# First cross-attention of a two-layer decoder: VectorE's instructions in written order, statistics and normalizations as steps of their own

## The chip, the cores and the metric

The kernel runs on one core of a Trainium2 chip, as one launch. A core has five engines with an instruction queue each: TensorE (PE, matrix products and transpositions), VectorE (DVE), ScalarE (ACT), GpSimd (POOL) and SyncE (SP), which here only issues DMA transfers. An engine works through its queue in order and waits on semaphores that other engines and transfers count up. The metric is the device time of one execution in microseconds (us), as the median of several runs; less is better.

## The reference, cut to what matters

The reference is two decoder layers on x of 16 batches x 112 tokens x 256 features. Each layer is `x + attention(norm(x))`, `x + cross_attention(norm(x), ctx)`, `x + ffn(norm(x))`. The change lies in the cross-attention of the first layer:

```
Q = (norm(x) @ W_Q + b_Q), K = (ctx @ W_K + b_K), V = (ctx @ W_V + b_V)   # 16 heads of 16
attn = softmax(Q K^T / sqrt(16));  out = (attn V) @ W_O + b_O;  x = x + out
```

The context has 375 rows a batch and is taken as it is. After this comes the first mixture of experts, which needs norm(x) of the result, router logits of it, and a shared expert; its shared expert and logits are computed inside the same stage. The second layer's cross-attention normalizes the same context; the mean and variance of each context row are worked out here already, and kept.

## The kernel before, in words

One stage handles the first cross-attention, about 154 to 572 us of the span. It loops over 16 batches b, and in each over four quads g, a quad being four heads. For a quad (b, g):

- `scores(b, g)`: four products of queries and keys (L614), each into a PSUM bank of its own, and on VectorE a negated maximum of each row (L616, tile mx).
- `shifted(b, g)`: TensorE transposes the maxima (L622), VectorE adds them to the queries (L624, tile qm).
- `weights(b, g, qm)`: the scores again, transposed and with the maxima taken off (L632), and ScalarE's exponential (L641).
- `values(b, g, pr)`: the products with V (L650), one quad behind.

While batch b is attended, batch b+1 is prepared: `prep(b + 1, part)` in quad `part` transposes the context and projects the queries (part 0, tile qn), the keys (part 1, tile kn), and the values (part 2). Queries and keys are then spread to 32-row groups (tiles qz and kz, two of each) by 16 small transfers each (`spread`, L554), all issued by SyncE; so is the context load (L224), two batches ahead. A batch thus takes 33 issues on SyncE. The tile cx has two buffers: a load waits until the batch two before it no longer needs its buffer.

In part 2, `prep` also takes the statistics of the context (L232 and L233 on VectorE into cmv, then two GpSimd instructions into cr). Quad 1 sets up `norm_one(lp, b + 2)`: statistics of x (L232, L233), GpSimd's power (L240, L241), the normalization (L236); the function that it returns, called in quad 3, transposes the result (L265, copied by L267 into xnT). `divide`, `out_T` and `out_proj` of batch b-1 follow in quads 1 to 3. `out_proj` adds the output to x (L687), and calls `norm_one` once more for the mixture of experts, into xrow; its transposition is put on the list `late` and taken in quad 1. A GpSimd add (L689) puts the normalized rows on x.

What sets the order: TensorE's is the order in which the Python loop calls things (`manual_schedule` with PE alone). The other engines' instructions are placed by a scheduler, which sorts by its own estimate of when each could start; each engine then keeps that order at run time. The next but one stage's instructions can be placed inside this one by it: the second layer's cross-attention loads its first two contexts into the same two cx buffers, and its normalization of them (L236, cx<-cx,cmv,cr) stands among this stage's VectorE instructions. PSUM is a pool of eight banks, used in turn: a TensorE step may have to wait until VectorE or ScalarE has read the bank of eight allocations before.

Of the kernel before, what the change touches and what calls it, by code (L numbers as in the profile page):

```python
# [20 lines left out]
NKC = S // KC  # L21
# [72 lines left out]
def tile_decoder(ctx: ExitStack, tc: tile.TileContext, t: dict, out: bass.AP):  # L94
# [135 lines left out]
    def stats_of(mv, src):  # L230
        st = sm.tile([src.shape[0], 6], F32, tag=f"st{src.shape[0]}", name="st", bufs=4)
        nc.vector.bn_stats(st, src)  # L232
        nc.vector.bn_aggr(mv, st)  # L233
# [4 lines left out]
    def rstd_pow(r, var):  # L238

        nc.gpsimd.tensor_scalar(r, var, EPS_LN, None, ALU.add)  # L240
        nc.gpsimd.tensor_tensor(r, r, power[: r.shape[0], : r.shape[1]], ALU.pow)  # L241

    def norm_one(lp, b, keep=None, affine=None, dst=None):


        if keep is None:
            mv = sm.tile([L, 2], F32, tag="nmv", name="nmv", bufs=4)
            r = sm.tile([L, 1], F32, tag="nr", name="nr", bufs=4)
        else:
            mv, r = keep[0][:, b, :], keep[1][:, b : b + 1]  # L250
        xn = lp.tile([L, D], F32, tag="xn", name="xn", bufs=2) if dst is None else dst
        stats_of(mv, x[:, b, :])
        rstd_pow(r, mv[:, 1:2])
        normed(xn, x[:, b, :], mv[:, 0:1], r)
        if affine is not None:
            mv2 = sm.tile([L, 2], F32, tag="nmv", name="nmv", bufs=4)
            r2 = sm.tile([L, 1], F32, tag="nr", name="nr", bufs=4)
            stats_of(mv2, xn)
            rstd_pow(r2, mv2[:, 1:2])
            normed(xn, xn, mv2[:, 0:1], r2)  # L260

        def to_xnT():
            pt = bank()
            for c in range(2):
                nc.tensor.transpose(pt[:, c * L : (c + 1) * L], xn[:, c * 128 : (c + 1) * 128], ident[:L, :L])  # L265
            if affine is None:
                nc.vector.tensor_copy(  # L267
                    xnT[:, :, b * L : (b + 1) * L], pt[:, : 2 * L].rearrange("p (c l) -> p c l", l=L)
                )
            else:  # L270
                for c in range(2):
                    nc.scalar.activation(
                        xnT[:, c, b * L : (b + 1) * L],
                        pt[:, c * L : (c + 1) * L],
                        AF.Identity,
                        bias=vec(affine[1] + c),
                        scale=vec(affine[0] + c),
                    )

        return to_xnT  # L280
# [247 lines left out]
    with ExitStack() as ph:  # L528
# [29 lines left out]
        def prep(b, part):  # L558
            if part == 0:
                if b + 2 < B:  # L560
                    cxs[b + 2] = load_ctx(b + 2)
                cT = lp.tile([128, 2, S], F32, tag="cT", name="cT", bufs=1)
                for c in range(2):
                    pt = bank()
                    for j in range(NKC):
                        nc.tensor.transpose(
                            pt[:, j * KC : (j + 1) * KC],
                            cxs[b][:, j, c * 128 : (c + 1) * 128],
                            ident[:KC, :KC],
                        )  # L570
                    nc.scalar.copy(cT[:, c, :], pt[:, :S])
                cTs[b] = cT
                nc.gpsimd.tensor_add(x[:, b, :], x[:, b, :], bo2[:, 1, :])
                qn = lp.tile([128, 2, L], F32, tag="qn", name="qn", bufs=1)
                pq = bank()
                for hf in range(2):
                    mm_sum(
                        pq[:, hf * L : (hf + 1) * L],
                        [(wq[:, c, hf * 128 : (hf + 1) * 128], xT(c, b)) for c in range(2)],
                    )  # L580
                for hf in range(2):
                    nc.vector.tensor_scalar(
                        qn[:, hf, :], pq[:, hf * L : (hf + 1) * L], vec(hf), 0.25, ALU.add, ALU.mult
                    )
                spread(qz[b % 2], qn)
            if part == 1:
                cT = cTs[b]
                kn = lp.tile([128, 2, S], F32, tag="kn", name="kn", bufs=1)
                for hf in range(2):
                    pk = bank()  # L590
                    mm_sum(pk[:, :S], [(wk[:, c, hf * 128 : (hf + 1) * 128], cT[:, c, :]) for c in range(2)])
                    nc.scalar.activation(kn[:, hf, :], pk[:, :S], AF.Identity, bias=vec(2 + hf), scale=1.0)
                spread(kz[b % 2], kn)
            if part == 2:
                cT = cTs.pop(b)
                for j in range(NKC):
                    pv = bank()
                    mm_sum(pv[:KC, :D], [(cT[:, c, j * KC : (j + 1) * KC], wv[:, c, :]) for c in range(2)])
                    nc.vector.tensor_tensor(
                        va[b % 2][:, j, :, :16],  # L600
                        pv[:KC, :D].rearrange("p (h d) -> p h d", d=16),
                        bV.rearrange("p (h d) -> p h d", d=16),
                        ALU.add,
                    )
                cx = cxs.pop(b)
                for j in range(NKC):
                    stats_of(cmv[:, b * NKC + j, :], cx[:, j, :])
                rstd_pow(cr[:, b * NKC : (b + 1) * NKC], cmv[:, b * NKC : (b + 1) * NKC, 1])

        def scores(b, g):  # L610
            ps = [bank() for _ in range(4)]
            for i in range(4):
                r = slice(32 * i, 32 * i + 32)
                mm(ps[i][:L, :S], qz[b % 2][r, g, :], kz[b % 2][r, g, :], start=True, stop=True)  # L614
            for i in range(4):
                nc.vector.tensor_reduce(  # L616
                    mx[b % 2][:, g, i, 16:17], ps[i][:L, :S], AX.X, ALU.max, negate=True
                )
# [65 lines left out]
        def out_proj(b, oT):  # L684
            po = bank()
            mm_sum(po[:L, :D], [(oT[:, c, :], wo[:, c, :]) for c in range(2)])
            nc.vector.tensor_add(x[:, b, :], x[:, b, :], po[:L, :D])  # L687
            late.append(norm_one(None, b, dst=xrow[:, b, :D]))
            nc.gpsimd.tensor_add(x[:, b, :], x[:, b, :], xrow[:, b, :D])  # L689

        late = []

        def logits(b):
            pl = bank()
# [19 lines left out]
                xb = x[:, b : b + 2, :].rearrange("p b d -> p (b d)")  # L714
                nc.vector.tensor_add(xb, xb, po[:L, :])

        with tc.manual_schedule(engines={mybir.EngineType.PE}):
            normq = {b: norm_one(lp, b) for b in range(2)}
            normq.pop(0)()
            normq.pop(1)()  # L720
            for part in range(3):
                prep(0, part)
            scores(0, 0)
            quads = [(b, g) for b in range(B) for g in range(NQ)]
            behind, oT = None, {}
            for n, (b, g) in enumerate(quads):
                if b + 1 < B and g < 3:
                    prep(b + 1, g)
                if b + 2 < B and g == 1:
                    normq[b + 2] = norm_one(lp, b + 2)  # L730
                if b + 2 < B and g == 3:
                    normq.pop(b + 2)()
                if b:
                    if g == 1 and late:
                        late.pop(0)()
                    if g == 2 and b > 1:
                        logits(b - 2)
                    if g == 1:
                        divide(b - 1)
                    if g == 2:  # L740
                        oT[b - 1] = out_T(b - 1)
                    if g == 3:
                        out_proj(b - 1, oT.pop(b - 1))
                qm = shifted(b, g)
                if n + 1 < len(quads):
                    scores(*quads[n + 1])
                pr = weights(b, g, qm)
                if behind is not None:
                    values(*behind)
                behind = (b, g, pr)  # L750
            a0 = shared_up(0)
            values(*behind)
            late.pop(0)()
            a1 = shared_up(1)
            divide(B - 1)
            shared_down(0, a0)
            logits(B - 2)
            oT = out_T(B - 1)
            a2 = shared_up(2)
            out_proj(B - 1, oT)  # L760
            shared_down(1, a1)
            shared_down(2, a2)
            late.pop(0)()
            logits(B - 1)
            a3 = shared_up(3)
            shared_down(3, a3)
# [704 lines left out]
```

## Time and profile before

| what | value |
|---|---|
| median of 3 runs | 1873.21 us (1871.97 to 1875.34) |
| profiled execution, its own time | 1875.62 us |
| its span, first to last instruction | 1873.8 us |
| mean granted TensorE clock | 0.942 |
| busy over the span | PE 1631.8, DVE 969.3, ACT 603.9, POOL 520.5 us |
| busy from 200 to 530 us (330 us of this stage) | PE 291.76, DVE 207.39, ACT 125.41, POOL 50.99 us |
| granted clock in those 330 us | 0.97 |

A line of the timeline gives the start in us from the span's beginning, the busy time, the engine (PEld is TensorE's weight load, SPq SyncE's DMA issue), the line of the kernel, the operation, output and input tiles, shapes, and how many were merged; in brackets how long the engine was idle just before, and what released it. In the list of waits a line names who waited, for whom, the total, how often, and the longest. SyncE's time in the profile is the issuing of a transfer, not its movement. Busy TensorE is not TensorE at its peak: the clock granted may be half of full speed.

### The profile page before, as it was taken

The numbers are of one execution on the slowest core, as the hardware profiler recorded it, in microseconds if no ns is written. First come the engines' busy times: TensorE is split into PE (matmuls) and PEld (weight loads), VectorE is DVE, ScalarE is ACT, GpSimd is POOL, SyncE is SP. The second block draws the span as 40 slices with busy tenths as digits, with TensorE's granted clock in tenths as the row PEclk, the third lists the DMA queues.
The fourth block names the chain that finished last, engine by engine and source line by source line (L and its number), as shares of the span: only waits on it lengthen the run. The fifth ranks groups of instructions, "written<-read, shape, count | busy, mean of one in ns | idle before, by whom it ended". The sixth has DMA issues, their size and how long they took to land. (4 is left out here: it accounts for less than half of the span.)

```text
span 1873.8 us, 31175 instructions
## 1 busy us (share of the span) xinstructions
PE 1631.8 (87%) x11755; PEld 1226.3 (65%) x11755; DVE 969.3 (52%) x2637; ACT 603.9 (32%) x1440; POOL 520.5 (28%) x699
## 2 busy tenths in 40 slices
PE   5877888898892496899999899999997999979992
PEld 4765666666661374778787566666665888868882
DVE  6864566666653243877776555655455432222222
ACT  2330334333430252223322334334342333313330
POOL 5532111111103452333333343534443000030003
PEclk9987899999996698999999999999998999999996
DMA  9401111111102345100000100000001244453422
GB/s 266 137 1 44 46 36 42 38 42 40 40 20 81 108 143 194 50 1 1 1 1 1 40 17 11 24 9 20 15 9 45 74 147 147 157 186 134 161 85 65
DMA packets 93342, 125.60 MB, mean 67 GB/s; under 512 B 17761, under 2 KB 76298, under 8 KB 93194
## 3 DMA queue, kind: packets, MB, share of 16 engines
q1 hardware_dynamic: 85178, 107.88, 18.7%
q0 software_dynamic: 5184, 13.13, 2.3%
q10 hardware_dynamic: 2832, 2.60, 0.5%
q8 instruction: 95, 1.56, 0.4%
q14 instruction: 53, 0.43, 0.1%
HBM read 94.40 MB, written 21.18 MB: 62 GB/s over the span
## 5 line engine op out<-in xcount | busy, mean ns | idle before, releaser
L1193 POOL TENSOR_SCALAR pr<-pr,den 112x375 f32<-112x375 f32 x128 | 156.3, 1239 | 197.7 <-DVE den L1191 191.7
L1373 DVE SCALAR_TENSOR_TENSOR hT<-pT,vT,gt 128x264 f32<-128x264 f32 x128 | 62.9, 492 | 242.3 <-ACT gt L1372 242.2
L115 PE MATMUL pT<-xnT,w_all 128*128 128x224 f32 (+2 forms) x736 | 163.4, 374 | 6.2 <-DVE xnT L267 6.2
L115 PEld LDWEIGHTS pT<-xnT,w_all 128*128 128x128 f32 x736 | 132.9, 196 | 25.0 <-issue 13.9
L641 ACT ACTIVATE pr<-pT 125x336 f32<-125x336 f32 x256 | 94.6, 456 | 167.8 <-PE pT L632 167.8
L1410 POOL DMA_INDIRECT got<-eo,row x32 | 30.4, 949 | 393.1 <-PE pT L115 215.4
L616 DVE TENSOR_REDUCE mx<-pT 112x1 f32<-112x375 f32 x256 | 125.7, 539 | 21.7 <-PE pT L614 21.0
L115 PE MATMUL pT<-cT,w_all 128*128 128x375 f32 x384 | 136.4, 496 | 0.2 <-ACT cT L1142 0.2
L115 PE MATMUL pT<-w_all,cT 128*125 128x256 f32 (+1 forms) x384 | 135.0, 495 | 0.0
L115 PE MATMUL pT<-hT,w_all 128*128 128x264 f32 x512 | 119.5, 392 | 6.4 <-ACT hT L1378 6.4
L115 PE MATMUL pT<-w_all 128*128 128x264 f32 x512 | 120.5, 392 | 0.0
L115 PE MATMUL pT<-e1T,w_all 128*128 128x264 f32 x512 | 119.1, 392 | 0.0
L115 PEld LDWEIGHTS pT<-hT,w_all 128*128 128x128 f32 x512 | 99.0, 194 | 24.2 <-ACT hT L1378 6.8
L1090 POOL TENSOR_TENSOR pr<-pr,den 112x448 f32<-112x448 f32 x64 | 59.3, 948 | 197.6 <-DVE den L1088 140.6
L115 PEld LDWEIGHTS pT<-e1T,w_all 128*128 128x128 f32 x512 | 98.4, 193 | 16.9
L115 PEld LDWEIGHTS pT<-w_all 128*128 128x128 f32 x512 | 98.2, 193 | 16.7
L115 PEld LDWEIGHTS pT<-cT,w_all 128*128 128x128 f32 x384 | 72.6, 194 | 53.1 <-issue 13.7
L115 PE MATMUL pT<-w_all,oT 128*112 128x256 f32 x448 | 106.4, 383 | 0.0
L115 PE MATMUL pT<-w_all,xnT 128*112 128x256 f32 (+1 forms) x320 | 103.8, 472 | 0.9 <-ACT xnT L390 0.9
L115 PEld LDWEIGHTS pT<-w_all,cT 128*125 128x125 f32 x384 | 70.9, 191 | 45.0 <-issue 31.8
L1372 ACT ACTIVATE gt<-pT,vT 128x264 f32<-128x264 f32 x128 | 61.4, 481 | 115.2 <-PE pT L115 92.4
L1182 ACT ACTIVATE pr<-pT,top 112x375 f32<-112x375 f32 x128 | 72.4, 573 | 52.1 <-DVE top L1181 50.1
(247 smaller groups left out, 3020.4 us busy)
## 6 DMA issues: line engine op xcount, KB each, us to landing
w_all<-in_L_ffn_w_c_fc_dram SPq DMA_DIRECT2D x16, 1024.0 KB
w_all<-in_L_ffn_w_gate_dram SPq DMA_DIRECT2D x16, 1024.0 KB
w_all<-in_L_ffn_w_c_proj_dram SPq DMA_DIRECT2D x16, 1024.0 KB
cx<-in_ctx_dram SPq DMA_DIRECT2D x32, 375.0 KB
kz<-kn SPq DMA_DIRECT2D x256, 23.4 KB
xg<-fill SPq DMA_DIRECT2D x1, 5547.0 KB
xb<-xg SPq DMA_DIRECT2D x43, 129.0 KB
eo<-os SPq DMA_DIRECT2D x16, 264.0 KB
```

The costliest lines, as they stand in the source:

```text
L115: mm(o, l, r, start=(i == 0), stop=(i == len(terms) - 1))
L616: nc.vector.tensor_reduce(mx[b % 2][:, g, i, 16:17], ps[i][:L, :S], AX.X, ALU.max, negate=True)
L641: nc.scalar.activation(pr[:, i, :], pw[i][:KC, : NKC * L], AF.Exp)
L1090: nc.gpsimd.tensor_tensor(pr[:, k], pr[:, k], bcast(den[:, k, :], L), ALU.mult)
L1182: nc.scalar.activation(pr[:, i, :], ps[i][:L, :S], AF.Exp, bias=top[:, i : i + 1], scale=1.0, accum_out=den[:, i : i + 1],)
L1193: nc.gpsimd.tensor_scalar(pr[:, n, :], pr[:, n, :], den[:, n : n + 1], None, ALU.mult)
L1372: nc.scalar.activation(gt, ps[1][:, :HS], AF.Identity, bias=vec(n_v + e * NJ + j), scale=1.0)
L1373: nc.vector.scalar_tensor_tensor(hT[:, j, :], ps[0][:, :HS], vec(12 + e * NJ + j), gt, ALU.add, ALU.mult)
L1410: nc.gpsimd.indirect_dma_start(out=got[:, :], out_offset=None, in_=eo[b // HB][:, :], in_offset=bass.IndirectOffsetOnAxis(ap=row[k][:, b : ...
```

## The change

VectorE's order in this stage becomes the order of the calls too (`manual_schedule` gets DVE beside PE). For that `norm_one` is taken apart into steps, and each is called at a place of its own:

- `stats(b)`: L232, L233 and the two GpSimd instructions; `norm(b)`: the normalization; `norm_T(b)`: transposition and copy to xnT; `out_norm(b)`: the normalization into xrow and the GpSimd add.
- `ctx_stats(b)`: the context's statistics, taken out of `prep(b, 2)`. For batch 0 it stands after the first scores; for b+1 behind the maxima that quad 2 of b issues.
- Within a quad the steps are called behind `scores` of the next quad: statistics of b+2 and `out_norm(b - 2)` in quad 0, `norm(b + 2)` in quad 1, `ctx_stats(b + 1)` in quad 2, `stats(b - 1)` in quad 3.
- `norm_T(b - 2)` moves into quad 1 with one batch more of delay for the output's normalization: its statistics are taken in quad 3 of the batch after, its normalization in quad 0 of the next.
- At the start `norm_T(1)` moves behind `prep(0, 0)`; at the end `shared_down(2, a2)` moves behind `norm_T(B - 1)`.

The instructions are the same in number and kind. Instructions of other stages are still placed by the scheduler, on VectorE too.

```diff
-                cx = cxs.pop(b)
-                for j in range(NKC):
-                    stats_of(cmv[:, b * NKC + j, :], cx[:, j, :])
-                rstd_pow(cr[:, b * NKC : (b + 1) * NKC], cmv[:, b * NKC : (b + 1) * NKC, 1])
+        def ctx_stats(b):
+            cx = cxs.pop(b)
+            for j in range(NKC):
+                stats_of(cmv[:, b * NKC + j, :], cx[:, j, :])
+            rstd_pow(cr[:, b * NKC : (b + 1) * NKC], cmv[:, b * NKC : (b + 1) * NKC, 1])
+
+        mvs, xns = {}, {}
+        def stats(b):
+            mv = sm.tile([L, 2], F32, tag="nmv", name="nmv", bufs=4)
+            r = sm.tile([L, 1], F32, tag="nr", name="nr", bufs=4)
+            stats_of(mv, x[:, b, :])
+            rstd_pow(r, mv[:, 1:2])
+            mvs[b] = mv, r
+
+        def norm(b, dst=None):
+            mv, r = mvs.pop(b)
+            xn = lp.tile([L, D], F32, tag="xn", name="xn", bufs=2) if dst is None else dst
+            normed(xn, x[:, b, :], mv[:, 0:1], r)
+            xns[b] = xn
+
+        def norm_T(b):
+            xn = xns.pop(b)
+            pt = bank()
+            for c in range(2):
+                nc.tensor.transpose(pt[:, c * L : (c + 1) * L], xn[:, c * 128 : (c + 1) * 128], ident[:L, :L])
+            nc.vector.tensor_copy(xnT[:, :, b * L : (b + 1) * L], pt[:, : 2 * L].rearrange("p (c l) -> p c l", l=L))
+
+        def out_norm(b):
+            norm(b, dst=xrow[:, b, :D])
+            nc.gpsimd.tensor_add(x[:, b, :], x[:, b, :], xrow[:, b, :D])
...
-            late.append(norm_one(None, b, dst=xrow[:, b, :D]))
-            nc.gpsimd.tensor_add(x[:, b, :], x[:, b, :], xrow[:, b, :D])
-
-        late = []
...
-        with tc.manual_schedule(engines={mybir.EngineType.PE}):
-            normq = {b: norm_one(lp, b) for b in range(2)}
-            normq.pop(0)()
-            normq.pop(1)()
-            for part in range(3):
-                prep(0, part)
+        with tc.manual_schedule(engines={mybir.EngineType.PE, mybir.EngineType.DVE}):
+            stats(0)
+            stats(1)
+            norm(0)
+            norm_T(0)
+            norm(1)
+            prep(0, 0)
+            norm_T(1)
+            prep(0, 1)
+            prep(0, 2)
             scores(0, 0)
+            ctx_stats(0)
...
                 if b + 1 < B and g < 3:
                     prep(b + 1, g)
-                if b + 2 < B and g == 1:
-                    normq[b + 2] = norm_one(lp, b + 2)
-                if b + 2 < B and g == 3:
-                    normq.pop(b + 2)()
+                if g == 1 and b > 1:
+                    norm_T(b - 2)
+                if g == 3 and b + 2 < B:
+                    norm_T(b + 2)
                 if b:
-                    if g == 1 and late:
-                        late.pop(0)()
...
                 qm = shifted(b, g)
                 if n + 1 < len(quads):
                     scores(*quads[n + 1])
+                if g == 0:
+                    if b + 2 < B:
+                        stats(b + 2)
+                    if b > 1:
+                        out_norm(b - 2)
+                if g == 1 and b + 2 < B:
+                    norm(b + 2)
+                if g == 2 and b + 1 < B:
+                    ctx_stats(b + 1)
+                if g == 3 and b:
+                    stats(b - 1)
                 pr = weights(b, g, qm)
...
+            out_norm(B - 2)
             a0 = shared_up(0)
             values(*behind)
-            late.pop(0)()
+            norm_T(B - 2)
...
             out_proj(B - 1, oT)
+            stats(B - 1)
             shared_down(1, a1)
+            out_norm(B - 1)
+            norm_T(B - 1)
             shared_down(2, a2)
-            late.pop(0)()
```

## The prediction

> **What bounds the kernel now.** The page's slices and the chain that ended last speak for the whole span; the change lies in one stage, 154 to 572 us. So I read the stage's waits, then the timeline of one batch, then the timeline of SyncE alone. The list of waits (200 to 540 us; total us, times, longest) names what holds VectorE and TensorE:
>
> ```profile
> DVE st L232 <- DMA cx<-in_ctx_dram: 41.6, 12, 5.6
> PE pT L265 <- DVE mx L616: 19.7, 10, 3.5
> PE pT L566 <- DVE mx L616: 7.6, 13, 0.6
> PE pT L632 <- DVE qm L624: 8.8, 12, 0.7
> ```
>
> VectorE waits 12 times for a context load. The timeline of a batch (start, us, engine, line) shows what is queued behind that wait:
>
> ```profile
> 301.09 0.92 PE L632 MATMUL pT<-qm,kz 32*125 32x112 f32 x24 [0.74 <-DVE qm L624]
> ...
> 306.53 0.43 DVE L232 BATCH_NORM_STATS2 st<-cx 125x6 f32<-125x256 f32 x1 [4.22 <-DMA cx<-in_ctx_dram]
> 306.87 0.53 DVE L616 TENSOR_REDUCE mx<-pT 112x1 f32<-112x375 f32 x1
> ...
> 307.46 0.41 PE L265 MATMUL pT<-call,xrow 112*128 112x112 f32 x2 [2.02 <-DVE mx L616]
> ```
>
> The fourth maximum stands behind statistics of a context still in flight, and TensorE stands 2.02 us behind that maximum. With the 0.74 and the 0.6 of L566, TensorE loses about 3.4 us of a batch of 23.2. Removing these looks like 14 x 3.4 = 48 us. But SyncE decides what can be kept:
>
> ```profile
> 300.87 0.42 SPq L224 DMA_DIRECT2D cx<-in_ctx_dram  x1
> 301.39 11.09 SPq L554 DMA_DIRECT2D qz<-qn  x16
> 312.58 10.37 SPq L554 DMA_DIRECT2D kz<-kn  x16
> 323.06 0.42 SPq L224 DMA_DIRECT2D cx<-in_ctx_dram  x1
> 324.12 12.06 SPq L554 DMA_DIRECT2D qz<-qn  x16
> ```
>
> It issues 33 transfers a batch with no pause. Each needs 0.63 us (0.587 and a gap of 0.045), some 1 to 1.8. From 185.5 (first qz of batch 1) to 510.6 (batch 15) a period is 325.2/14 = 23.2 us. Idle gaps over 0.1 us in SyncE's timeline sum to 11.7. Of these 6.2 lie ahead of the first qz of a batch (1.19, 0.12, 1.75, 0.57, 0.90, 0.21, 0.16, 1.33), waiting for qn; 5.5 lie inside runs and come from transfers. A batch's first scores need the fourth kz, which lands 1.3 us after its issue; they follow that landing by -0.4 to 3.4 us. SyncE is a second bound right behind TensorE.
>
> The last lines concern the next stage's context, which the scheduler normalizes here (L236):
>
> ```profile
> 510.12 0.42 SPq L224 DMA_DIRECT2D cx<-in_ctx_dram  x1
> ...
> 516.28 0.41 DVE L236 TENSOR_SCALAR cx<-cx,cmv,cr 125x256 f32<-125x256 f32 x1 [5.45 <-DMA cx<-in_ctx_dram]
> ...
> 517.21 0.41 PE L265 MATMUL pT<-call,xrow 112*128 112x112 f32 x2 [3.48 <-DVE mx L616]
> ...
> 532.64 0.32 PE L622 MATMUL pT<-call,mx 112*128 112x112 f32 x1 [1.54 <-DVE mx L616]
> ```
>
> It is issued as soon as kz of batch 14 is done, VectorE waits 5.45 us, TensorE 3.48.
>
> **The Trainium skill.** "DVE: scalar operands, raw-bit mode, write accounting and state across instructions" (Flops that outlive an instruction) says the vector queue is one in-order queue; the trace agrees: maxima whose scores are ready stand 4.2 us behind a waiting instruction. "Perfetto Trace Analysis" (What "DMA-bound" means) names a sequencer full of DMA slices as a bound of its own; SyncE above agrees. "TensorE: Matmul & The Clock Gate" (What's actually happening) lets the clock fall to half after an idle window of some 3.4 us; the trace agrees: TensorE idles 3.3 us until 192.1, and the slice 192 to 196 has clock 0.50.
>
> **The change, part by part.** I use the order of instructions in the compiled changed program; its times are from the rows above.
>
> *Steady part.* Statistics of a context (three L232 of 0.4 us, three L233 of 0.17) now belong to the context one batch ahead, which landed long before. Statistics of x and the normalization are a quad apart, which covers the 1.0 us of GpSimd's power. Ahead of qn stand only four maxima and one L232/L233. All three waits go. What comes instead: context statistics (1.7 us) stand ahead of qm of the fourth quad, whose matmuls wait about 1.1 us for it. TensorE's own pace becomes 23.2 - 3.4 + 1.1 = 20.9 us; SyncE's floor is (325.2 - 6.2)/14 = 22.8. So SyncE bounds and only its qn waits go: -6.2. At the start qn(0) no longer stands behind context statistics: first matmuls end at 163.0, qn at 163.4 rather than 164.1: -0.7. kz of batch 14, finished at 510.0 before, is finished at 503.1.
>
> *The two hoisted loads.* A context buffer is free only after its statistics, so the scheduler sets every context load one place later in SyncE's order. The next stage's first load (batch 0) comes after kz(14), its second after kz(15). But VectorE has their L236 early:
>
> ```
> SyncE:   kz(14) x16 | cx' 0 | qz(15) x16 | kz(15) x16 | cx' 1
> VectorE: qm(13,3) | L236 cx' 0 | mx(14,0) x2 | L236 | mx x2 | L232 | L236 | L233 | qn(15) x2
> VectorE: qm(14,3) | mx(15,0) x1 | L236 cx' 1 | mx x2 | L236 | mx x1 | L232 | L236 | L233 | qm(15,0)
> ```
>
> mx(14,0) can start when the fourth kz(14) has landed, but stands behind a load that is issued after the sixteenth. No deadlock: kz needs nothing of VectorE. First stall: from the end of kz(14), issue 0.1, landing 5.6 (5.3 to 6.7 in this stage, one early load at 7.4), L236 and first maximum 1.0; then TensorE does values 0.78, six transposes 1.1, projection 1.15 for batch 15; qn and signals 0.55: 10.3 us until the first qz(15), against 0.6 before (510.02 to 510.64): +9.7. TensorE has then idled some 11 us, so its three steps run at half clock, as at 180 to 194 us (1.35, 1.5, 1.9): +1.7.
>
> Batch 15's 32 issues then run with no load just ahead: 32 x 0.63 and one long one, 21.3 against 22.65 before: -1.3.
>
> Second stall: from the end of kz(15), 0.1 + 5.6, then L236, two maxima, L236, one maximum: 2.3. The transposition of mx(15,0) starts 8.0 after that end; before, it started 0.65 ahead of it (532.64 against 533.29): +8.7. TensorE is idle about 10 us and restarts at half clock; after the idle time up to 192.1 this lasted to 197.8, so 5.7 us at half cost 2.9: +2.9. From here TensorE alone sets the end.
>
> *Tail.* In the last batch no projection covers out_norm(13), which now stands behind four maxima: xrow is 1.0 us late for L265 and delays the next qm: +1.2. At the end norm_T(15) waits behind one shared_down instead of two: +0.5. Later stages have the same order on every engine and shift as a whole; the xb fetches behind the second load wait for routing anyway.
>
> Sum: -6.2 - 0.7 + 9.7 + 1.7 - 1.3 + 8.7 + 2.9 + 1.7 = +16.5 us. The profiled execution took 1875.6 (span 1873.8), so it would take 1892.1; the median of the runs stands 2.4 below it: 1889.7.
>
> Unknown: GpSimd's and ScalarE's order hardly changes and is costed at nothing; both idle most of the stage (51 and 125 us busy of 330), and even 1 us late they stand behind SyncE's slack of 1.9 us a batch. Gaps inside SyncE's runs could shrink too, by 5.5 at most; or the qn waits stay: 6.2 back. Half clock: 0 to 7 for both stalls together, I take 4.6.
>
> **Rivals.**
> 1. *Stalls as worked out, SyncE's stream no faster.* The statistics ahead of qm and SyncE's uneven issues meet, and the period stays at 23.2. For it: TensorE's margin is only 1.9 us. Against: qn has nothing slow ahead of it. 16.5 + 6.2 = +22.7: 1895.9.
> 2. *Smaller stalls.* The clock stays full (4.6 less) and gaps inside the runs go too (5.5 less): +6.4: 1879.6. For it: 5.45 us of waiting at 516 cost only one half-clock window of 3.4 us. Against: the idle times are now twice as long.
> 3. *Faster.* The two loads do not stand in the way. Then SyncE gives 6.9, and the last batch, whose scores lagged the landing by 2.8 us, gives 1.5 more: about 1865. One mechanism decides: L236 must find its data. The load would have to be issued 12 us earlier (seven for the twelve kz behind the fourth, 5.6 for landing), before kz(14). The compiled order says otherwise.
> 4. *No difference:* stalls of about 4 us each, as before; needs the load six us ahead of kz's end.
>
> **How the numbers follow.** Forecast 0.62 (1884 to 1894), rival 1 0.12, rival 2 0.16, rival 3 0.07, rival 4 0.03. A measurement of this kernel tells 0.2%, 3.7 us. Rivals 1 and 2 are slower too: slower 0.90, same 0.03, faster 0.07. The range 1880 to 1896.5 runs from rival 2 to rival 1.
>
> **What would show it.** L232 of cx waits for no load; L265 and qm waits gone from the list; SyncE without gaps ahead of qz up to batch 14; kz(14) finished near 503. Then L236 idle before it about 10 us twice, followed by TensorE idle over 8 us and clock 0.5, qz(15) near 515 and the stage ending some 16 us later. Wrong if the L236 waits are under 6 us, if SyncE still pauses ahead of qz, or if kz(14) ends past 508.

## The result, and the profile after

The changed kernel takes 1883.85 us (median of 22 runs, 1879.10 to 1892.43), the kernel before beside it 1874.24 (22 runs, 1870.00 to 1884.66): a ratio of 1.0053, 95% interval 1.0040 to 1.0065, so about 10 us slower. The forecast was 1889.7 with a range of 1880 to 1896.5.

The profiled execution of the changed kernel took 1879.71 us (span 1877.9), which is below its median by 4.1, that of the kernel before 1875.62, which is above its own by 1.4. So the two profiles lie only 4.1 us apart. Part of what they lack against the 9.6 us between the medians is scatter outside the change: over all kernels of this study the first transposition of the self-attention (L491) comes at 37.4 to 41.0 us, and the program behind this stage takes 1300.3 to 1303.4 us; the changed kernel's profile has the lowest value of both, together 3.1 us less than the profile of before.

In the code of the changed kernel the maxima are L645, their transposition L651, qm L653, scores L643 and L661, values L679. Its list of waits, 200 to 545 us (who waited for whom: total us, times, longest), answers to the list of before:

```profile
DVE cx L236 <- DMA cx<-in_ctx_dram: 23.1, 2, 13.6
PE pT L679 <- DVE mx L645: 10.5, 1, 10.5
PE pT L651 <- DVE mx L645: 10.4, 1, 10.4
PE pT L643 <- DMA kz<-kn: 9.2, 9, 1.7
PE pT L661 <- DVE qm L653: 5.0, 18, 0.9
```

The 41.6 us that L232 waited for loads are gone, and so are the waits for a maximum at the transpositions. Two single waits stand in their place, and a new small one: TensorE now waits for the keys (kz), which are SyncE's transfers. The timeline shows the two large ones with what is behind them (start, us, engine, line; idle time and its releaser in brackets):

```profile
497.26 0.41 SPq L224 DMA_DIRECT2D cx<-in_ctx_dram  x1
502.81 0.41 DVE L236 TENSOR_SCALAR cx<-cx,cmv,cr 125x256 f32<-125x256 f32 x1 [13.56 <-DMA cx<-in_ctx_dram]
503.74 1.35 PE L679 MATMUL pT<-pr,va 125*32 125x112 f32 x24 [10.54 <-DVE mx L645]
...
508.46 10.28 SPq L554 DMA_DIRECT2D qz<-qn  x16
...
518.84 10.37 SPq L554 DMA_DIRECT2D kz<-kn  x16
...
529.31 0.42 SPq L224 DMA_DIRECT2D cx<-in_ctx_dram  x1
535.02 0.41 DVE L236 TENSOR_SCALAR cx<-cx,cmv,cr 125x256 f32<-125x256 f32 x1 [9.57 <-DMA cx<-in_ctx_dram]
...
537.18 0.45 PE L651 MATMUL pT<-call,mx 112*128 112x112 f32 x1 [10.41 <-DVE mx L645]
```

Each load is issued right behind the last kz, VectorE stands at L236 until it has landed (5.5 and 5.7 us), and TensorE idles over 10 us each time. The SyncE timeline of the changed kernel shows what bounds the batches ahead of it:

```profile
312.97 0.42 SPq L224 DMA_DIRECT2D cx<-in_ctx_dram  x1
314.03 11.34 SPq L554 DMA_DIRECT2D qz<-qn  x16
325.46 11.44 SPq L554 DMA_DIRECT2D kz<-kn  x16
337.01 0.40 SPq L224 DMA_DIRECT2D cx<-in_ctx_dram  x1
```

It issues almost without a pause, as before. The mean period over batches 1 to 13 is 22.85 us, against 23.21 before.

The steps of the prediction can be laid beside the two profiles (us from the span's start; the last column adds up the prediction's terms):

| moment | before | after | difference | predicted |
|---|---|---|---|---|
| last transposition of the self-attention (L491) | 136.0 | 130.7 | -5.3 | 0 |
| first qz | 164.19 | 156.73 | -7.5 | -0.7 |
| kz(14) finished | 510.02 | 497.16 | -12.9 | -6.9 |
| qz(15) starts | 510.64 | 508.46 | -2.2 | +4.5 |
| kz(15) finished | 533.29 | 529.21 | -4.1 | +3.2 |
| transposition of mx(15,0) | 532.64 | 537.18 | +4.5 | +11.9 |
| end of the stage (last addition of the shared expert) | 571.33 | 577.61 | +6.3 | +16.5 |

From row to row the predicted differences hold within 1 us, but for the first two rows and the last: the stage starts 7.5 us early where 0.7 was expected, and its end adds 1.7 where 4.6 were expected.

That gain lies ahead of the stage. In the kernel before, the scheduler had put the context statistics of batches 0 and 1 (six L232, L233, and GpSimd's L240 and L241) into the first self-attention. Its timeline there:

```profile
55.06 0.42 DVE L232 BATCH_NORM_STATS2 st<-cx 125x6 f32<-125x256 f32 x1
...
57.95 0.41 PE L491 MATMUL pT<-call,a 112*128 112x112 f32 x2 [1.10 <-POOL a L484]
...
63.65 0.89 POOL L241 TENSOR_TENSOR cr<-cr,power 125x3 f32<-125x3 f32 x1
...
64.50 0.72 POOL L484 TENSOR_TENSOR a<-a 112x256 f32<-112x256 f32 x1
65.28 0.41 PE L491 MATMUL pT<-call,a 112*128 112x112 f32 x2 [1.46 <-POOL a L484]
```

The same transposition in the changed kernel, whose written order holds these statistics in their own stage:

```profile
56.18 0.41 PE L491 MATMUL pT<-call,a 112*128 112x112 f32 x2 [0.29 <-POOL a L484]
...
62.35 0.41 PE L491 MATMUL pT<-call,a 112*128 112x112 f32 x2 [0.29 <-POOL a L484]
```

A batch of the self-attention takes 6.2 us there instead of 7.3, because VectorE and then GpSimd (L484) have nothing foreign ahead of what TensorE waits for.

### The profile page after: what moved, and what is told of

Same layout as the page of the kernel before. It is cut to its first block, busy times and chain, and to the rows that moved or that the text cites. A ratio compares the mean times of both kernels' runs of the same rounds, so it can differ in the third digit from the quotient of the medians.

```text
span 1877.9 us, 31401 instructions
## 1 busy us (share of the span) xinstructions
PE 1648.7 (88%) x11755; PEld 1241.6 (66%) x11755; DVE 975.0 (52%) x2637; ACT 603.7 (32%) x1440; POOL 520.8 (28%) x699
## 5 line engine op out<-in xcount | busy, mean ns | idle before, releaser
L115 PEld LDWEIGHTS pT<-xnT,w_all 128*128 128x128 f32 x736 | 137.6, 205 | 24.1 <-issue 14.6
L645 DVE TENSOR_REDUCE mx<-pT 112x1 f32<-112x375 f32 x256 | 124.3, 541 | 26.1 <-PE pT L643 23.2
L115 PEld LDWEIGHTS pT<-e1T,w_all 128*128 128x128 f32 x512 | 97.5, 192 | 16.5
L115 PEld LDWEIGHTS pT<-cT,w_all 128*128 128x128 f32 x384 | 72.7, 195 | 53.1 <-issue 11.6
L643 PE MATMUL pT<-kz,qz 32*112 32x375 f32 x512 | 80.8, 541 | 14.8 <-DMA kz<-kn 14.8
## 6 DMA issues: line engine op xcount, KB each, us to landing
kz<-kn SPq DMA_DIRECT2D x256, 23.4 KB
```

The source lines that it names most:

```text
L115: mm(o, l, r, start=(i == 0), stop=(i == len(terms) - 1))
L645: nc.vector.tensor_reduce(mx[b % 2][:, g, i, 16:17], ps[i][:L, :S], AX.X, ALU.max, negate=True)
```

## The experiments

The theory: (1) two stalls of L236 behind late context loads cost about 21 us; (2) SyncE's issuing bounds the batches in both kernels, so little of VectorE's gain is kept; (3) the start gains some 7 us because no context statistics stand in the self-attention. The rival to each stands in the expectations. Times are medians. Each group of runs had runs of the kernel before beside it (1874.88 for the first four, 1873.58 for the next four, 1875.05 for the last two); at the ratio 1.0053 the changed kernel is at 1884.8 and 1883.5 beside the first two groups.

### The two stalls, both and one

```diff
-                for j in range(NKC):
-                    n = b * NKC + j
-                    normed(cxs[b][:, j, :], cxs[b][:, j, :], cmv[:, n, 0:1], cr[:, n : n + 1])
+                with tc.issue_after(last[0]) if b in (0, 1) else ExitStack():
+                    for j in range(NKC):
+                        n = b * NKC + j
+                        normed(cxs[b][:, j, :], cxs[b][:, j, :], cmv[:, n, 0:1], cr[:, n : n + 1])
```

`last[0]` is the first cross-attention's last addition of the shared expert (L740 in the changed kernel). The second run has `b in (1,)`.

> The changed kernel, with the next stage's normalization of its contexts 0 and 1 (six L236) placed behind this stage's last VectorE instruction, so that no maximum stands behind a late context load. Theory (two stalls): the pause of SyncE between kz(14) and qz(15) falls from 11.3 to about 1 us, TensorE reaches the transposition of mx(15,0) at the end of kz(15) instead of 8.0 us after it, the half clock goes; the six L236 cost up to 2.5 us in the routing: 17 to 22 us less than the changed kernel, 8 to 12 less than the kernel before. Rival (the stalls cover each other or other work, and something else made the change slower): within 5 us of the changed kernel.

> As the run before, but only context 1's three L236 are moved: the first stall stays (the L236 of context 0 waits some 13.6 us, SyncE pauses about 11 us), the second goes. Theory: 8 to 12 us less than the changed kernel, about half of what both together give, so the stalls add up. Rival (a single stall moves TensorE as far as both): less than 3 us from either the changed kernel or the run before.

Measured: 1863.78 us with both moved, ratio to the kernel before 0.9943 (0.9929 to 0.9958), so 21 us less than the changed kernel and 11 less than the kernel before. With only the second moved 1872.94, ratio 0.9992 (0.9983 to 1.0002), 12 us less than the changed kernel. So the first stall is worth 9 us (between the two runs) and the second 12. With both moved, the timeline shows no L236 at this place:

```profile
496.58 0.41 SPq L224 DMA_DIRECT2D cx<-in_ctx_dram  x1
497.09 11.48 SPq L555 DMA_DIRECT2D qz<-qn  x16
...
515.16 0.45 PE L652 MATMUL pT<-call,mx 112*128 112x112 f32 x1
...
519.08 0.42 SPq L224 DMA_DIRECT2D cx<-in_ctx_dram  x1
```

qz(15) starts 0.6 us after kz(14) instead of 11.3, and the transposition of mx(15,0) precedes the end of kz(15) by 3.8 us instead of following it by 8.0. With one moved, the first stall stands as it was:

```profile
500.81 0.41 SPq L224 DMA_DIRECT2D cx<-in_ctx_dram  x1
506.49 0.41 DVE L236 TENSOR_SCALAR cx<-cx,cmv,cr 125x256 f32<-125x256 f32 x1 [12.41 <-DMA cx<-in_ctx_dram]
...
511.68 10.98 SPq L555 DMA_DIRECT2D qz<-qn  x16
```

(The line numbers of this stage are one higher in these two runs: the maxima are L646, their transposition L652.) Theory 1 holds, and the stalls add up. The six L236 now stand in the routing behind the stage; the program behind the stage takes 1302.0 us with them, within the scatter of the other kernels.

### The same edit on the kernel before

> The kernel before, with the same six L236 moved behind the stage. Theory: it has the same stalls in small (TensorE 3.5 us behind the first, 1.5 us behind the second) while the rest of its stream is bound by VectorE's waits and SyncE: 0 to 5 us less than the kernel before. Rival (the normalizations in that place are what bounds the end of the stage in either kernel): 15 us less or more.

Measured: 1873.82 us, ratio 0.9997 (0.9986 to 1.0009). Its own waits of L236 (4.12 and 5.45 us) cost the kernel before nothing that can be told. There qz(15) starts 0.6 us after kz(14) with the six L236 in place and 0.7 without them. So the edit is worth 21 us only in the order of the changed kernel, where the L236 hold qn(15), and with it SyncE.

### The context statistics of the first two batches

On the changed kernel they are put back into the self-attention, there at the steps for batches 4 and 5:

```diff
+                if i in (4, 5):
+                    ctx_stats0(i - 4)
...
         def ctx_stats(b):
             cx = cxs.pop(b)
+            if b < 2:
+                return
```

> The changed kernel, with the context statistics of batches 0 and 1 taken inside the first self-attention stage again, as the kernel before had them. Theory (the start gain of 7.5 us comes from these six L232 and their GpSimd steps no longer standing in the self-attention): the last transposition of that stage comes 5 to 8 us later, and the kernel takes 5 to 8 us more than the changed one. Rival (the gain comes from the rewritten start of the cross-attention itself): 0 to 1 us more.

Measured: 1890.86 us, ratio 1.0092 (1.0075 to 1.0108), 6 us more than the changed kernel. The last L491 comes at 137.7 us instead of 130.7, the first qz at 163.70 instead of 156.73. This puts them closer together than the scheduler had done, so it shows that the place costs some 6 us, not that every spread of them would.

The other way round, on the kernel before, they are held back in this stage (`put` is the last addition of values, L599):

```diff
-                for j in range(NKC):
-                    stats_of(cmv[:, b * NKC + j, :], cx[:, j, :])
+                with tc.issue_after(put.ins) if b < 2 else ExitStack():
+                    for j in range(NKC):
+                        stats_of(cmv[:, b * NKC + j, :], cx[:, j, :])
```

> The kernel before, with the context statistics of batches 0 and 1 held back behind the addition of their own values (L599), so that none of them stands in the first self-attention; the loads and L236 at the end of the stage keep their order. Theory (these six L232 and their GpSimd steps cost the self-attention about 7 us): its first qz is issued at 156 to 160 us instead of 164, and the kernel takes 5 to 8 us less than the kernel before. Rival (the earlier start is lost again, because SyncE's stream or the late statistics of the first two contexts hold the first batches): 0 to 2 us less.

Measured: 1879.50 us, ratio 1.0019 (1.0007 to 1.0031), about 4 us more where 5 to 8 less were expected: a miss, and worse than its rival, which expected 0 to 2 less. The start did come earlier (first qz 159.92), but VectorE then met another load set late in SyncE's order. The timeline of this run:

```profile
203.40 0.41 SPq L224 DMA_DIRECT2D cx<-in_ctx_dram  x1
203.87 0.54 SPq L554 DMA_DIRECT2D kz<-kn  x1
209.24 0.43 DVE L232 BATCH_NORM_STATS2 st<-cx 125x6 f32<-125x256 f32 x1 [12.76 <-DMA cx<-in_ctx_dram]
...
211.06 1.61 PE L633 MATMUL pT<-qm,kz 32*125 32x112 f32 x24 [12.10 <-DVE cmv L233]
```

With the statistics later, their buffer comes free later; the scheduler set a load behind fifteen of the sixteen kz of batch 1 (L224 at 203.40), while VectorE's order still had the statistics of that context early. One batch takes 35.4 us instead of 22. It is the stall of the changed kernel at another place.

A measure that this doesn't touch is the time from the first to the last L491 of the self-attention: 93.0 to 93.4 us in the seven kernels without context statistics in it (the changed one and six of the experiments; 93.3 in the run just told), 97.3 to 99.5 in the five with them (97.7 before). So their place costs the self-attention 4 to 6 us, and theory 3 holds for the larger part of the gain. A further 1 to 2 lies between the last L491 and the first qz: 28.2 us before, 26.0 after, and 25.9 to 27.5 in the experiments. This part does not come from the statistics in the self-attention: the changed kernel with them put back there has 26.0 too. What it comes from was not tested by itself.

### Half the issues on SyncE

The sixteen transfers of a spread become eight of twice the size (groups g and g+2 have the same partitions); bytes and row lengths stay.

```diff
-            for g in range(NQ):
+            for r in range(2):
                 for i in range(4):
-                    p = 64 * (g % 2) + 16 * i
-                    nc.sync.dma_start(dst[32 * i : 32 * i + 16, g, :], src[p : p + 16, g // 2, :])
+                    p = 64 * r + 16 * i
+                    nc.sync.dma_start(dst[32 * i : 32 * i + 16, r::2, :], src[p : p + 16, :, :])
```

> The changed kernel, with each pair of spreading transfers of the same partitions (groups g and g+2) merged into one of twice the size: 16 issues a batch on SyncE in place of 32, the same bytes. Theory (SyncE's issuing bounds the steady part of the changed kernel at some 22.7 us a batch, TensorE alone would need about 20.9): SyncE pauses in every batch, 14 x 1.8 = 25 us go, and the first of the two stalls shrinks by up to 5 us because fewer issues stand between the fourth kz and the context load: 25 to 36 us less than the changed kernel. Rival (TensorE or VectorE sets the pace): 0 to 5 us less. Second rival (the transfers' movement is what is waited for): no gain or a loss, as the merged ones move twice the rows each.

> Both edits on the changed kernel: the six L236 behind the stage, and 16 spreading issues a batch in place of 32. Theory: the two causes add up: about 25 us (18 to 32) less than the run with the L236 moved alone, some 1832 to 1846 us, with a period of 20.5 to 21.5 us a batch. Rival (TensorE-bound already): within 5 us of the run with the L236 moved alone.

> The kernel before, with 16 spreading issues a batch in place of 32. Theory (its VectorE waits for context loads that SyncE issues late, and SyncE itself bounds it): loads are issued earlier, the twelve waits of VectorE for a load shrink, 10 to 40 us less than the kernel before. If VectorE's own order with its waits were the bound: within 5 us of the kernel before.

Measured: on the changed kernel 1837.37 us, ratio 0.9814 (0.9789 to 0.9838), 46 less. With the L236 moved as well 1821.74, ratio 0.9739 (0.9716 to 0.9763), 42 less than with the L236 moved alone by the medians, 38 by the two ratios. On the kernel before 1836.90, ratio 0.9813 (0.9793 to 0.9834), 37 less. In each of these three pairs VectorE's order in the profiles is the same, instruction by instruction. SyncE now pauses in every batch (changed kernel with both edits):

```profile
301.15 5.33 SPq L555 DMA_DIRECT2D kz<-kn  x8
310.95 0.27 SPq L224 DMA_DIRECT2D cx<-in_ctx_dram  x1
316.02 6.17 SPq L555 DMA_DIRECT2D qz<-qn  x8
322.28 6.01 SPq L555 DMA_DIRECT2D kz<-kn  x8
331.63 0.27 SPq L224 DMA_DIRECT2D cx<-in_ctx_dram  x1
```

From batch 3 on the period is 20.69 us, to 0.01 us, where it had wandered between 22.0 and 23.6. On the kernel before it becomes 21.15. Theory 2 holds for both kernels, and more strongly than stated: the order of VectorE is worth 0.46 us a batch once SyncE is out of the way, and the issues 2.1. The waits of TensorE's L265 for a maximum, 19.7 us in all in the kernel before, are no longer in its list with half the issues, although VectorE's order is the same.

The first two of these runs gained more than was expected. Between the first qz and the transposition of mx(15,0) lie 358.5 us with the L236 moved alone and 320.1 with half the issues as well, 38 less. Some 11 of it come from the first two periods (14.90 and 18.72 against 21.17 and 23.51), in which SyncE had paused for only 0.1 and 0.9 us ahead of qz; the estimate had counted only the steady batches. Up to the end of the stage the two profiles lie 41.8 us apart: the last 3.4 are a stretch of half clock in the run with 32 issues (last section). In the run on the changed kernel alone the two stalls also shrink: with 332.1 between the same two points it has 12 us of stalls over the run with both edits, where the changed kernel with its 380.5 has 22 over the run with the L236 moved. Its L236 waits 4.5 and 4.3 us.

### The steps moved, VectorE's order left to the scheduler

```diff
-        with tc.manual_schedule(engines={mybir.EngineType.PE, mybir.EngineType.DVE}):
+        with tc.manual_schedule(engines={mybir.EngineType.PE}):
```

> The steps split and moved as in the changed kernel, but VectorE's order left to the scheduler (TensorE's alone written). The compiled order takes the context statistics of batches 0 and 1 into the first self-attention stage again, and sets the L236 of the next contexts behind maxima. Theory: the 6 to 7 us of the start are lost, the two stalls are as small as in the kernel before (3 to 6 us each), SyncE bounds the steady part: 1866 to 1880 us. Rival (the moved steps alone make the stalls): 1885 us or more.

Measured: 1871.73 us, ratio 0.9991 (0.9981 to 1.0002), no difference from the kernel before. L232 waits for loads again (12 times, 46.4 us from 200 to 510 us), the first qz comes at 163.17, the period is 22.98, and from kz(14) to qz(15) there are 0.6 us. So it is the written order of VectorE, not the splitting and moving of the steps, that brought both the gain at the start and the stalls.

### The statistics ahead of qm

With SyncE out of the way, the prediction's remaining term can be measured: the three statistics of a context stand ahead of the fourth quad's qm, for which the prediction added 1.1 us a batch. Here they are spread over quads 0 to 2, on the kernel with both edits:

```diff
-                if g == 2 and b + 1 < B:
-                    ctx_stats(b + 1)
+                if g < 3 and b + 1 < B:
+                    ctx_stats(b + 1, [g])
```

> The run with both edits (L236 behind the stage, 16 spreading issues a batch), with the three context statistics spread over quads 0, 1 and 2 instead of all behind the maxima of quad 2. Theory (with SyncE out of the way, the 1.7 us of statistics ahead of qm of the fourth quad cost TensorE about 0.9 us a batch): the period falls from 20.69 to 19.8 to 20.4 us, 4 to 12 us less. Rival (the wait only moves to the other quads' qm, or something else sets the period): within 2 us.

Measured: 1808.61 us, ratio 0.9639 (0.9611 to 0.9666), 13 us less by the medians, a little more than the 4 to 12 expected; the period is 19.65. The list of waits from 200 to 470 us, ahead of it:

```profile
PE pT L662 <- DVE qm L654: 13.7, 26, 0.9
```

and in this run (the same two lines of the code, two further down):

```profile
PE pT L664 <- DVE qm L656: 2.0, 13, 0.2
```

The waits for qm go down by 11.7 us in this window, about 0.9 a batch; 14 periods of 1.03 less give 14.4 us. This is the fastest kernel of the study, 3.6% faster than the kernel before.

## Why the prediction was right, and where it was not

**Sign and mechanism: right.** The next stage's normalization, set ahead of maxima in VectorE's written queue, met loads that SyncE issues only behind kz. Moving the six instructions away, and nothing else, takes 21 us off. The number is inside the range, but in part by the range's width: two terms missed by 5.8 and 2.9 us in the same direction (below), so +9.6 us was measured where +16.5 was forecast. It lies nearer to the second rival's figure than to the forecast, without that rival's reasons.

**First stall: right.** +9.7 and +1.7 of half clock were predicted up to the start of qz(15), and -1.3 for the issues of batch 15. The profiles show +10.7 and -1.9; the timed runs give 9 for this stall as a whole, against 10.1.

**Second stall: right.** +8.7 was predicted, the transposition of mx(15,0) moved by +8.6 against the end of kz(15). The timed runs give 12 for the stall with its half clock, against 11.6.

**Half clock after it, and the tail: too large.** 2.9 and 1.7 were added. From the transposition of mx(15,0) to the stage's end the kernel before takes 38.7 us, the changed one 40.4, and the run with the second stall removed, which has full clock there, 39.3. So by these three profiles the half clock cost about 1.1 and the tail 0.6. The clock was back at full speed some 5 us after the restart.

**Steady part: right in sum, not in detail.** -6.2 was predicted by taking away all of SyncE's waits for qn; from qz(1) to the end of kz(14) there are 319.3 us instead of 324.6, -5.3. The gaps of over 0.2 us ahead of a qz fall from 6.6 to 2.6 us and are not quite gone. The sizes that decided this term came out: SyncE's floor of 22.8 us a batch is the 22.85 measured, TensorE's own pace of 20.9 shows as 20.69 once SyncE issues half as often, and the 1.1 us of statistics ahead of qm are the 1.03 that spreading them takes off.

**The start: the step that failed.** "At the start qn(0) no longer stands behind context statistics: ... -0.7" should have been -6.5: 4.3 in the self-attention and 2.2 between it and the first qz (another 1.0 of the 7.5 in this pair of profiles is scatter of the first transposition, 38.4 against 37.4). The prediction took its own sentence "the change lies in one stage, 154 to 572 us" as given and looked for moved instructions behind that stage only. The statistics of the first two contexts stood ahead of it, at 53 to 74 us, in the profile of before. With -6.5 in place of -0.7, and 1.7 for half clock and tail in place of 4.6, the sum is +7.8, where the medians differ by 9.6 and the interval of the ratio reaches from 7.5 to 12.

**What bounds the kernel: the order was the wrong way round.** The prediction called TensorE with its waits the first bound, SyncE "a second bound right behind TensorE". With half the issues the kernel before runs at 21.15 us a batch with the same order on VectorE. So about 2.1 of the 3.4 us a batch that TensorE lost in waits were SyncE's lateness, passed on through the loads and through VectorE: the wait of L265, 1.3 us a batch over the window of its list, goes. How the rest divides was not measured. The page "Perfetto Trace Analysis" of the Trainium skill (What "DMA-bound" means) names a full sequencer as a bound, and that is what these runs show; it then says that large descriptors are what matter. Here the rows kept their length and only the number of transfers was halved, and SyncE's time for a spread fell from about 11 to 5.5 us (medians).

**The rivals.** The first (SyncE's stream no faster) fell: it gained 5.3. The second (full clock, no gaps) was half right: the clock cost less, the gaps stayed. The fourth needed small stalls. The third, that the loads do not stand in the way, put the kernel at about 1865: the run with the L236 moved has 1863.8. Its condition was not met in the changed kernel, and once it is met by moving the L236, the closeness is in part luck: that run also starts 6 us earlier than the rival had it, and loses over 3 us to half clock at its end.

## What to carry to other kernels

When one engine's order is fixed by hand, follow every instruction that the fixed block lets in or keeps out, ahead of the stage as much as behind it: the scheduler fills neighbours' gaps across stages, and both the gain here (statistics that left the self-attention) and the loss (normalizations that came in from the next stage) were of other stages. A wait at the head of an in-order queue holds all that stands behind it (here at a cost of 21 us in one order of VectorE, and of nothing measurable in another), so an instruction whose load is issued late belongs behind the last urgent one, not where a gap seems free. And before waits are reordered, ask what issues the thing that is waited for: halving SyncE's transfers was worth about four times the difference that the new order made.

## What the runs showed of the hardware that was not expected

- In these runs an issue on SyncE is paid by the transfer, not by its size: a kz transfer takes 0.58 us with 23.4 KB and 0.59 with 46.9 KB, a qz transfer 0.54 with 7.0 KB and 0.59 with 14.0 KB (medians, changed kernel, and with half the issues), the context load with 375 KB 0.42. A spread of eight takes about 5.5 us instead of 11 for sixteen.
- In the run with the L236 moved, the clock fell to half from 514 to 524 us, although TensorE's only idle time in the ten microseconds before that was 0.70 us; its scores then came one by one behind the kz transfers. Three windows of it (start and end, length, busy us and instructions of PE, PEld, DVE, ACT and POOL, granted clock, share of the DMA engines, GB/s):

```profile
510.00:511.00 1.00, 0.45 (x2) 0.27 (x2) 0.93 (x5) 0.00 (x0) 0.08 (x1) 1.00 0.13 32
511.00:512.00 1.00, 1.00 (x5) 0.39 (x4) 0.85 (x3) 0.00 (x0) 0.92 (x2) 1.00 0.19 47
514.00:515.00 1.00, 1.00 (x24) 0.83 (x24) 0.45 (x2) 1.00 (x4) 0.34 (x2) 0.51 0.18 46
```

  It is no single case. From 200 to 510 us this run has six more such stretches, of 3.4 or 6.9 us, and each starts 1 to 4 us after a batch's first scores had waited 0.5 to 1.8 us for kz. With half the issues as well, the granted clock is 1.00 from 200 to 460 us; over the whole program it is 0.948 to 0.951 in that kernel's six runs, and 0.935 to 0.939 in the five of the run with the L236 moved. The page "TensorE: Matmul & The Clock Gate" (What's actually happening) of the Trainium skill speaks of an idle window of some 3.4 us; no idle time here is that long. What TensorE's activity must be to keep the clock stays open. Most of these stretches lie where SyncE sets the pace; the last one, from the transposition of mx(15,0) to the stage's end, cost about 3.4 us (42.8 against 39.3 in the run with one stall).
- Restarts at half clock after idle times of over 10 us lasted only some 4 to 5 us, and the second cost about 1.1. In both cases the clock had fallen before the long wait or early in it: at 490.7 us with TensorE idle from 493.2, and at 528.3 with TensorE idle from 526.8.
